# Interleaved pairs of scan tiles, buffers in small pieces, and a table that breaks the planner's ties

## The chip, the cores and the metric

The kernel runs on one NeuronCore of one Trainium2 chip. The metric is the device time of one execution in microseconds (us), the median of several runs. Everything is float32. TensorE (PE in the profile) multiplies matrices into PSUM; VectorE (DVE), ScalarE (ACT) and GpSimd (POOL) work on vectors; SyncE (SP) issues the transfers between the device memory and the on-chip memory SBUF.

## What is computed

Eight images of 384 channels and 1024 positions go through a Mamba-like block and then, the first five of them, through a feed-forward block with binarised weights (the last three have a zero feed-forward output). Cut to what matters:

```
t  = layernorm(x)                               # over the 384 channels, per position
xm, z = split(t @ in_proj_w.T)                  # 768 channels each
xc = silu(causal_conv3(xm))
dt, Bm, Cm = split(xc @ x_proj_w.T, [24, 16, 16])
dt = softplus(dt @ dt_proj_w.T + dt_proj_b)     # 768 channels
h[d,n](l) = exp(dt*A) * h[d,n](l-1) + (dt*xc)[d] * Bm[n](l)   # 768 channels x 16 states
y[d](l)   = sum_n h[d,n](l) * Cm[n](l) + xc*D
x += gelu((y * silu(z)) @ out_proj_w.T @ mlp_w1.T + b1) @ mlp_w2.T + b2
# images 0..4: groupwise sign of the weights, groupwise absmax quantisation
h = quant(layernorm(x) @ sign(W1 - mean) + b1);  x += quant(gelu(h) @ sign(W2 - mean) + b2)
```

## The kernel before

The positions lie along the free dimension of SBUF, channels along the 128 partitions. An image `b` has three stages. `s1` does the norm, the input projections, the convolution and the dt projection, in two halves of 512 positions, and hands `xc`, `z`, `dt`, `dt*xc` (`dtx`) and the rows of B and C to the scan through device memory. `s2` is the scan. `s3` does the output projection and the MLP; `ffn` is the feed-forward block of images 0 to 4, `binarise` its weights.

**The scan.** A tile of 128 partitions holds 32 channels times 4 states (a "quad" `q`, four quads for 16 states). For the six middle images a tile has all 1024 positions; for the first and the last image the halves are done apart, with two groups of channels side by side (`wide` = 2). Two tiles make a unit `m`. In `scan_tile` each tile takes: `exp` on ACT into `da` (PSUM); `u = dtx * B` on POOL (line 886); the scan instruction on DVE (line 890); the product by C, in place on POOL (line 904) or on DVE (line 907), as `on_pool` says; and matmuls with the matrix `fold` (line 842), which sum the states into the PSUM tile `py`. These matmuls are 32 columns wide, and four of them stand side by side in the array. They are issued for two quads at a time, 16 records in the profile (a float32 matmul makes two). `dt_r` and `dtx_r` are loaded with each channel row repeated over four partitions.

**The order.** Nothing is issued by hand. All operations are put into a `Plan` with an engine, a cost, the tiles read and written and a lane; `Plan.run` walks through a model of time, takes for each engine an operation that could start, and emits it. Where several could start, `rank` decides: scan first (lane 0 and the sums in lane -1), then the other stages by lane and image, and within those by the sequence number `op.prio[2]` in which the operations were written down. Each engine then runs its instructions in the order emitted. Where PE would idle for more than 0.7 us in the plan, small matmuls `spare` (line 412) are put in to keep its clock up.

**The buffers.** Each kind of tile has a ring of buffers, and an operation can start only when a buffer is free. The wide ones hold 6 x 512 columns: `front` (2; `xc`, `dt`, `z` of `s1`), `hid` (2; hidden layer of the MLPs), `yg` (1). Silu, softplus and Gelu run over such a tile in one instruction of 3072 columns. `u` has 9 tiles, `dt_r` and `dtx_r` 3 each, `sq` (the square of the norm) 1, `mm` 3 PSUM tiles for all matmul outputs but the scan's. The matmuls of the projections are all emitted by `matmuls` (line 494). `p_dt` (line 722) is the dt projection, 24 real rows padded to 128; `p_bc` (line 703) picks the rows of B and C, in four matmuls of 128 columns, out of `dbc`.

Of the kernel before, what the change touches and what calls it, by code (L numbers as in the profile page):

```python
# [26 lines left out]
F32 = mybir.dt.float32  # L27
# [6 lines left out]
P = 128  # L34
# [8 lines left out]
HK = KH // 2  # L43
T = 512
# [41 lines left out]

def c_act(n):
    return 0.25 + n * 0.00084


def c_dve(n):
    return 0.19 + n * 0.00102


def c_pool(n):
    return 0.18 + n * 0.00214
# [33 lines left out]
class Piece:  # L130
# [8 lines left out]

    def __getitem__(self, part):  # L140
        return self, part

# [20 lines left out]
class Plan:  # L163
# [57 lines left out]
    def run(self):  # L221
# [22 lines left out]
        def choose(e, now, able):  # L244
# [9 lines left out]
            return min(able, key=rank)  # L254

        def rank(op):
# [11 lines left out]
            return (*first, op.prio[2])  # L268
# [83 lines left out]
class Layer:  # L352
    def __init__(self, ctx, tc, a, out):
# [9 lines left out]
        def ring(tag, bufs, where=sbuf):  # L363
# [7 lines left out]
            "front": ring("front", 2), "t_f": ring("t_f", 2), "w_f": ring("w_f", 3),  # L371
            "dbc": ring("dbc", 1), "halo": ring("halo", 2),

            "dt_r": ring("dt_r", 3), "dtx_r": ring("dtx_r", 3), "u": ring("u", 9),
# [4 lines left out]
            "yg": ring("yg", 1), "hid": ring("hid", 2), "t_b": ring("t_b", 1), "w_b": ring("w_b", 3),  # L379
            "w6": ring("w6", 2), "w6_n": ring("w6_n", 2), "res": ring("res", 2),  # L380

            "t_n": ring("t_n", 2), "small": ring("small", 7),
# [9 lines left out]
        for b in range(B):  # L392
            for name in ("dt", "dtx"):
                self.dram[name, b] = handed(f"{name}_d{b}", [DI, L])
# [24 lines left out]

    def constants(self):
# [13 lines left out]
        self.pick = const.tile([P, 2 * NS], F32, name="pick")  # L436
        nc.vector.tensor_add(self.pick, ident[:, DQ : 2 * DQ], ident[:, DP + DQ : DP + 2 * DQ])
        self.edge = const.tile([P, KD, 2], F32, name="edge")
# [50 lines left out]
    def matmuls(self, p, w, t, k0, n, start, stop, r, claim, w0=0):  # L489


        def emit():
            for k in range(n):
                self.nc.tensor.matmul(  # L494
                    p.real, w.real[:, w0 + k, :], t.real[:, k0 + k, :],
# [102 lines left out]
    def s1(self, b):  # L598
# [6 lines left out]
        def by_pair(name, half, t):  # L605
            d = self.dram[name, b]
            self.store(d.real[:, half].rearrange("k p l -> p k l"), t, lambda x: x, [d[half]],
                       4 * P * KD * T)

        def tiled(name, half, t):  # L610
            d = self.dram[name, b]
            to = d.real[:, HALVES[half]].rearrange("(k p) l -> p k l", p=P)
            self.store(to, t, lambda x: x, [d[half]], 4 * P * KD * T)
# [14 lines left out]
        def gate(half, t):  # L628
            z = self.piece(r_z, [P, KD, T], "z")
            for m in range(KD):  # L630
                w = self.weights(r_w, KC, a["in_proj_w"][KD + m])
                pm = self.mm3(w, t, [t[k] for k in range(KC)], [z], "p_z")
                self.affine(
                    lambda m=m, z=z: z.real[:, m, :], lambda pm=pm: pm.real, [pm], [z[m]]
# [637 lines left out]
```

## Time and profile before

| | |
|---|---|
| median of 3 runs | 3261.88 us (3261.76 to 3268.25) |
| profiled execution: time, span | 3262.23 us, 3260.4 us |
| mean granted TensorE clock | 0.984 |
| moved by DMA | 748.73 MB, 230 GB/s |
| first POOL product of the scan starts, last one starts | 105.1 us, 3166.5 us |

The span runs from the first to the last instruction of the program; the time has some 1.8 us more around it. An engine's busy time is the sum of its instructions' durations without overlap. In the rows of the profile, `out<-in` are the program's tile names, `x768` is the count, and behind the bar stand the busy total in us, the mean of one in ns, and the idle time just before with what ended it.

### The profile page before, as it was taken

How to read it: one execution, taken by the hardware profiler on the slowest of the kernel's cores; microseconds unless marked ns; L12 is line 12 of the kernel's file. 1: busy time of each engine (PE TensorE's matmuls, PEld its weight loads, DVE VectorE, ACT ScalarE, POOL GpSimd, SP SyncE). 2: the span in 40 equal slices, each digit the busy share in tenths (PEclk: the TensorE clock that was granted, in tenths of full speed). 3: DMA queues.
4: the chain of work that ended last, by engine and by line, in shares of the span. 5: the costliest groups of instructions: out<-in, count | busy, mean ns of one | idle time of the engine just before them, and what ended most of it. 6: DMA issues, size and time to landing. Idle time of an engine off the chain costs nothing.

```text
span 3260.4 us, 34027 instructions
## 1 busy us (share of the span) xinstructions
PE 3122.5 (96%) x11098; PEld 1317.7 (40%) x11098; DVE 2742.3 (84%) x2127; ACT 2024.3 (62%) x2246; POOL 2848.7 (87%) x1371
## 2 busy tenths in 40 slices
PE   8988999999999999999899999999999999999999
PEld 4333433444433434334334344343443534433334
DVE  4778899799978899888998878999788988789880
ACT  4778787656665576665656566755666565656551
POOL 1688899979999989999989999989999899999970
PEclk9998999999999999999999999999999999999999
DMA  6988778657796568675686667866677656766542
GB/s 218 305 282 276 249 250 294 221 183 234 259 322 197 184 230 291 229 238 197 208 298 211 237 211 246 295 225 226 220 275 250 207 185 205 249 187 207 167 141 76
DMA packets 367345, 748.73 MB, mean 230 GB/s; under 512 B 33856, under 2 KB 111168, under 8 KB 367168
## 3 DMA queue, kind: packets, MB, share of 16 engines
q1 hardware_dynamic: 366736, 746.46, 68.5%
q8 instruction: 89, 1.46, 0.2%
q14 instruction: 88, 0.72, 0.1%
q10 hardware_dynamic: 432, 0.09, 0.0%
HBM read 566.06 MB, written 180.36 MB: 229 GB/s over the span
## 4 chain that ended last, share of the span: by engine, by line
PE 74%; DMA 9%; DVE 6%; ACT 5%; issue 2%; POOL 2%; SPq 1%; ACTq 0%; DVEq 0%; POOLq 0%
PE p_y L494 17%; PE p_o L494 14%; PE p_h L494 13%; PE py L842 9%; PE p_out L494 6%; PE p_z L494 6%; PE p_in L494 5%; DVE da L890 2%; DMA w<-in_out_proj_w 2%; DMA w_f<-in_in_proj_w 2%; DVE u L890 1%; ACT L510 1%; DMA w_b<-in_mlp_w 1%; ACT da L510 1%; PE spare L412 1%
## 5 line engine op out<-in xcount | busy, mean ns | idle before, releaser
L886 POOL TENSOR_TENSOR u<-dtx_r,bc 128x1024 f32<-128x1024 f32 x768 | 1790.4, 2362 | 72.3 <-DMA dtx_r<-dtx_d 46.3
L510 ACT ACTIVATE da<-dt_r,a_neg 128x1024 f32<-128x1024 f32 (+1 forms) x960 | 902.7, 945 | 534.0 <-DVE u L907 331.1
L904 POOL TENSOR_TENSOR u<-u,bc 128x1024 f32<-128x1024 f32 x352 | 828.4, 2364 | 121.5 <-DVE u L890 115.5
L890 DVE TENSOR_TENSOR_SCAN da<-da,u 128x1024 f32<-128x1024 f32 (+1 forms) x416 | 840.5, 2020 | 111.6 <-POOL u L886 62.9
L890 DVE TENSOR_TENSOR_SCAN u<-da,u 128x1024 f32<-128x1024 f32 (+1 forms) x352 | 699.5, 2010 | 90.3 <-ACT da L510 63.0
L494 PE MATMUL p_h<-t,w_b 128*128 128x512 f32 x1152 | 513.6, 600 | 10.9 <-DMA w_b<-in_mlp_w 9.9
L907 DVE TENSOR_TENSOR u<-da,bc 128x1024 f32<-128x1024 f32 x416 | 507.9, 1221 | 10.5 <-ACT state L901 0.3
L494 PE MATMUL p_o<-g,w 128*128 128x512 f32 x1152 | 506.7, 595 | 5.4 <-ACT g L510 2.9
L842 PE MATMUL py<-u,fold 128*32 128x512 f32 x3072 | 376.6, 605 | 4.5 <-DVE u L907 4.5
L494 PEld LDWEIGHTS p_h<-t,w_b 128*128 128x128 f32 x1152 | 214.7, 190 | 298.1 <-issue 256.4
L494 PEld LDWEIGHTS p_o<-g,w 128*128 128x128 f32 x1152 | 215.9, 190 | 292.0 <-issue 277.3
L494 PE MATMUL p_y<-tn,w_b 128*128 128x512 f32 x720 | 324.9, 598 | 4.0 <-DVE tn L592 3.3
L494 PE MATMUL p_y<-gf,w_n 128*128 128x512 f32 x720 | 319.0, 599 | 6.7 <-DMA w_n<-bin_w 4.0
L510 ACT ACT_TABLE_LOAD x222 | 284.8, 1283 | 11.7 <-DVE xc L661 7.3
L494 PE MATMUL p_out<-yg,w 128*128 128x512 f32 x552 | 249.2, 604 | 8.9 <-DMA w<-in_out_proj_w 4.3
L494 PE MATMUL p_z<-t,w_f 128*128 128x512 f32 x504 | 232.5, 611 | 8.2 <-DMA w_f<-in_in_proj_w 6.2
L494 PE MATMUL p_in<-t,w_f 128*128 128x512 f32 x504 | 228.3, 602 | 10.8 <-DMA w_f<-in_in_proj_w 8.6
L494 PEld LDWEIGHTS p_y<-gf,w_n 128*128 128x128 f32 x720 | 135.1, 191 | 187.6 <-issue 172.4
L494 PEld LDWEIGHTS p_y<-tn,w_b 128*128 128x128 f32 x720 | 133.9, 190 | 183.9 <-issue 155.4
L842 PEld LDWEIGHTS py<-u,fold 128*32 128x32 f32 x3072 | 81.5, 110 | 261.1 <-issue 203.2
L525 ACT ACTIVATE g<-p_h,v_vecs 128x512 f32<-128x512 f32 x157 | 106.3, 681 | 120.9 <-PE p_h L494 120.7
L525 ACT ACTIVATE y<-p_y,v_vecs 128x512 f32<-128x512 f32 x138 | 94.1, 683 | 130.0 <-PE p_y L494 100.3
(112 smaller groups left out, 2700.3 us busy)
## 6 DMA issues: line engine op xcount, KB each, us to landing
dtx_r<-dtx_d SPq DMA_DIRECT2D x144, 512.0 KB, 5.8
dt_r<-dt_d SPq DMA_DIRECT2D x144, 512.0 KB, 6.0
w_b<-in_mlp_w SPq DMA_DIRECT2D x192, 192.0 KB, 2.9
w<-in_mlp_w SPq DMA_DIRECT2D x96, 384.0 KB, 3.6
w_f<-in_in_proj_w SPq DMA_DIRECT2D x168, 192.0 KB, 4.2
y_d<-y SPq DMA_DIRECT2D x120, 256.0 KB, 3.4
gf<-y_d SPq DMA_DIRECT2D x20, 1536.0 KB, 9.5
xc_d<-xc SPq DMA_DIRECT2D x16, 1536.0 KB, 7.3
```

The lines of the kernel that those rows point to most:

```text
L412: self.plan.fill = lambda: self.nc.tensor.matmul(self.plan.spare.real[:, : 2 * P], self.ones, self.one.to_broadcast([P, 2 * P]), start=Tru ...
L494: self.nc.tensor.matmul(p.real, w.real[:, w0 + k, :], t.real[:, k0 + k, :], start=start and k == 0, stop=stop and k == n - 1,)
L510: lambda: self.nc.scalar.activation(out(), in_(), func, **{k: v() if callable(v) else v for k, v in kw.items()}),
L525: nc.scalar.activation(out(), in_(), AF.Identity, bias=bias, scale=scale)
L842: nc.tensor.matmul(py.real[p0 : p0 + DQ, :], self.fold, hc, start=False, stop=(q == NQUAD - 1), skip_group_check=True,)
L886: add("POOL", 2.36, lambda: nc.gpsimd.tensor_mul(u.real, dtx_r.real, spread(bq)), r=[dtx_r, bq], w=[u])
L890: add("DVE", (0.2 if half else 0.15) + n * 0.00209, lambda k=k, col=col: nc.vector.tensor_tensor_scan(to.real[:, k, :], da.real[:, k, :], ...
L904: add("POOL", 2.36, lambda: nc.gpsimd.tensor_mul(u.real, u.real, spread(cq)), r=[cq], w=[u])
L907: add("DVE", 1.21, lambda: nc.vector.tensor_mul(u.real, da.real, spread(cq)), r=[da, cq], w=[u])
```

## The change

- **Interleaved pairs.** A unit's two tiles become one pair. `u` and `dtx_r` hold `[128, n, 2]`, the two tiles' values alternating; `s1` writes `dtx` to device memory in this form. One POOL instruction multiplies the pair by the row of B, repeated for both (step 0 in the innermost dimension), one more by the row of C. DVE's scan reads `u` with a step of two elements, and writes it so where C is multiplied on POOL; where C is multiplied on DVE, that product is written with a step of two. The `fold` matmuls read `u` with a step of two. For the last quad the product is written over `dtx_r` itself. Channels are grouped so that a pair's two tiles are in the same partitions of neighbouring 128-row blocks (the weights are laid out on the host to suit). `on_pool` changes which quads have C multiplied on POOL.
- **Small pieces.** `front`, `hid` and `yg` become rings of pieces of 2 x 512 columns (`Split`): 7, 6 and 3 of them. Silu, softplus, Gelu, clip, stores and loads go piece by piece. `res` goes from 2 to 4, `u` from 9 tiles to 3 pairs, `dtx_r` from 3 tiles to 2 pairs, `small` from 7 to 5.
- **Projections.** `p_bc` is replaced by one matmul with the matrix `join`, which gives the dt rows twice, at partitions 0 and 32, and the rows of B and C in one block that one DMA stores. The dt projection then uses 32 rows of the array per matmul, two at a time. `binarise` sums the weights in four column strips and reduces by group on DVE.
- **Ties.** `rank` adds to the sequence number a number between -16 and 16, made from it and from an entry of `TURNS`, one per 100 us of planned time; where the entry is 0, nothing is added.

```diff
+STRETCH, REACH = 100, 16
+TURNS = (
+    0, 0, 0, 7221, 34335, 0, 0, 0, 0, 0, 13486, 57910,
+    29230, 27985, 0, 0, 0, 0, 13021, 0, 59942, 28281, 23998, 0,
+    35936, 26840, 53796, 0, 0, 45431, 13885,
+)
+def turned(n, by):
+    x = ((n + 1) * 2654435761 + by * 40503 * 65537) & 0xFFFFFFFF
+    x = ((x ^ x >> 15) * 2246822519) & 0xFFFFFFFF
+    return (x ^ x >> 13) % (2 * REACH + 1) - REACH
...
+def c_pair(n):
+    return 0.19 + n * 0.00188
...
+class Split:
+    def __init__(self, make, n, per):
+        self.pieces, self.per = [make() for _ in range(n // per)], per
+    def at(self, k):
+        return self.pieces[k // self.per].real[:, k % self.per, :]
+    def __getitem__(self, k):
+        return self.pieces[k // self.per][k % self.per]
...
-            return min(able, key=rank)
-
-        def rank(op):
+            at = int(now / STRETCH)
+            turn = TURNS[at] if at < len(TURNS) else 0
+            return min(able, key=lambda op: rank(op, turn))
+        def rank(op, turn):
...
-            return (*first, op.prio[2])
+            return (*first, op.prio[2] + (turned(op.prio[2], turn) if turn else 0))
...
-            "front": ring("front", 2), "t_f": ring("t_f", 2), "w_f": ring("w_f", 3),
+            "front": ring("front", 7), "t_f": ring("t_f", 2), "w_f": ring("w_f", 3),
...
-            "dt_r": ring("dt_r", 3), "dtx_r": ring("dtx_r", 3), "u": ring("u", 9),
+            "dt_r": ring("dt_r", 3), "dtx_r": ring("dtx_r", 2), "u": ring("u", 3),
...
-            "yg": ring("yg", 1), "hid": ring("hid", 2), "t_b": ring("t_b", 1), "w_b": ring("w_b", 3),
-            "w6": ring("w6", 2), "w6_n": ring("w6_n", 2), "res": ring("res", 2),
-
-            "t_n": ring("t_n", 2), "small": ring("small", 7),
+            "yg": ring("yg", 3), "hid": ring("hid", 6), "t_b": ring("t_b", 1), "w_b": ring("w_b", 3),
+            "w6": ring("w6", 2), "w6_n": ring("w6_n", 2), "res": ring("res", 4),
+            "t_n": ring("t_n", 2), "small": ring("small", 5),
...
+        def in_place(t, func, table):
+            parts = [t[k] for k in range(KD)]
+            for p, piece in enumerate(t.pieces):
+                mine = parts[p * PER : (p + 1) * PER]
+                self.act(lambda piece=piece: piece.real, lambda piece=piece: piece.real, func,
+                         c_act(PER * T), r=parts if p == 0 else mine, w=mine, table=table)
...
+            p_all = self.piece("mm", [P, T], "p_all")
+            n_all = DP + 2 * NS
+            add("PE", MM, lambda dbc=dbc, p_all=p_all: nc.tensor.matmul(
+                p_all.real[:n_all, :], self.join, dbc.real, start=True, stop=True
+            ), r=[dbc], w=[p_all])
             self.affine(
-                lambda rows=rows: rows.real, lambda p_bc=p_bc: p_bc.real, [p_bc], [rows], n=TG
+                lambda dbc=dbc: dbc.real[:n_all, :], lambda p_all=p_all: p_all.real[:n_all, :],
+                [p_all], [dbc],
             )
             d = self.dram["rows", b]
-            for g in range(G):
-                at = slice(cols.start + g * TG, cols.start + (g + 1) * TG)
-                self.store(d.real[:, at], rows, lambda x, g=g: x[g * DQ : (g + 1) * DQ, :],
-                           [d[half, g]], 4 * DQ * TG)
-            dt = self.piece(r_x, [P, KD, T], "dt")
-            for k in range(KD):
-                if k % KC == 0:
+            self.store(d.real[:, cols], dbc, lambda x: x[DP:n_all, :], [d[half]], 4 * 2 * NS * T)
...
+                def two(k=k, pds=pds, dbc=dbc, ws=ws):
+                    for i in range(2):
+                        rows = slice(i * DQ, (i + 1) * DQ)
+                        nc.tensor.matmul(
+                            pds[i].real, ws[i].real[rows, (k + i) % KC, :], dbc.real[rows, :],
+                            start=True, stop=True,
+                        )
+                add("PE", MM + 0.2, two, r=[dbc, *dict.fromkeys(ws)], w=pds, claim=[dt.pieces[k // PER]])
...
+            d = self.dram["dtx", b]
+            for p in range(KC):
+                dtx = self.piece("sq", [P, T, 2], "dtx")
+                add("POOL", 2.35, lambda p=p, dtx=dtx, xc=xc, dt=dt: nc.gpsimd.tensor_mul(
+                    dtx.real.rearrange("p n i -> p i n"), xc.pieces[p].real, dt.pieces[p].real
+                ), r=[xc[2 * p], xc[2 * p + 1], dt[2 * p], dt[2 * p + 1]], w=[dtx])
+                self.store(d.real[p, :, half * L : (half + 1) * L], dtx,
+                           lambda x: x.rearrange("p n i -> p (n i)"), [d[p, half]], 4 * P * L)
...
+            dtxs = self.piece("dtx_r", [P, wide, n, 2], "dtx_r")
+            d = self.dram["dtx", b]
+            at = 2 * cols.start
+            for x in range(wide):
+                src = d.real[p, r0 + x :: G, at : at + 2 * n].unsqueeze(1)
+                load(dtxs[x], lambda x=x, t=dtxs: t.real[:, x].rearrange("p n i -> p (n i)"),
+                     src.to_broadcast([DQ, SQ, 2 * n]), [d[p, h] for h in halves], 8 * P * n)
...
+                u = dtxs if q == NQUAD - 1 else self.piece("u", [P, wide, n, 2], "u")
...
+                        parts = [u.real[:, 0, h, i] for i in both for h in HALVES] if (
+                            half is None) else [u.real[:, x, :, i] for i in both for x in both]
+                        for g, hc in enumerate(parts):
                             nc.tensor.matmul(
-                                py.real[p0 : p0 + DQ, :], self.fold, hc,
+                                py.real[g * DQ : (g + 1) * DQ, :], self.fold, hc,
                                 start=False, stop=(q == NQUAD - 1), skip_group_check=True,
...
-    def on_pool(self, i, q, m):
-
-        return q == 0 or (q == 2 and (i == 0 or m % 3))
...
+    def on_pool(self, q, m):
+        return q % 2 == 0 or (q == 1 and m % 4 == 0)
...
+        def product(t, x, row):
+            nc.gpsimd.tensor_mul(
+                u.real[:, x], t.real[:, x], row.real.unsqueeze(2).to_broadcast([P, n, 2])
             )
-        add("POOL", 2.36, lambda: nc.gpsimd.tensor_mul(u.real, dtx_r.real, spread(bq)),
-            r=[dtx_r, bq], w=[u])
-        to = u if on_pool else da
-        for k, col in enumerate(cols):
-            add("DVE", (0.2 if half else 0.15) + n * 0.00209, lambda k=k, col=col: nc.vector.tensor_tensor_scan(
-                to.real[:, k, :], da.real[:, k, :], u.real[:, k, :],
-                state.real[:, col : col + 1] if half else 0.0, ALU.mult, ALU.add,
-            ), r=[da, u] + ([state[cols[0]]] if half else []), w=[to])
-        if half == 0:
-            c0, step = cols[0], cols[1] - cols[0]
-            kept, last = lambda: state.real[:, c0 : c0 + step + 1 : step], n - 1
-            if on_pool:
-                add("POOL", 0.2, lambda: nc.gpsimd.tensor_copy(kept(), to.real[:, :, last]),
-                    r=[to], w=[state[c0]])
-            else:
-                add("ACT", 0.16, lambda: nc.scalar.copy(kept(), to.real[:, :, last]),
-                    r=[to], w=[state[c0]])
+        for x in range(wide):
+            add("POOL", c_pair(2 * n), lambda x=x: product(dtxs, x, bq), r=[dtxs[x], bq],
+                w=parts[x])
...
+            to = (lambda i: in_u(i)) if on_pool else (
+                lambda i, da=da: da.real[:, i, :])
+            for i, col in enumerate(mine):
+                add("DVE", (0.2 if half else 0.15) + n * 0.00209, lambda i=i, col=col, to=to,
+                    da=da, in_u=in_u: nc.vector.tensor_tensor_scan(
+                        to(i), da.real[:, i, :], in_u(i),
+                        state.real[:, col : col + 1] if half else 0.0, ALU.mult, ALU.add,
+                    ), r=[da, u[t]] + ([state[col]] if half else []),
+                    w=[u[t] if on_pool else da])
...
+                def by_dve(t=t, da=da):
+                    row = cq.real.unsqueeze(1)
+                    if wide == 1:
+                        nc.vector.tensor_mul(u.real[:, 0, :, t], da.real[:, 0, :], cq.real)
+                    else:
+                        nc.vector.tensor_mul(
+                            u.real[:, t].rearrange("p n i -> p i n"), da.real,
+                            row.to_broadcast([P, wide, n]),
+                        )
+                add("DVE", 1.21, by_dve, r=[da, cq], w=[u[t]])
         if on_pool:
-            add("POOL", 2.36, lambda: nc.gpsimd.tensor_mul(u.real, u.real, spread(cq)),
-                r=[cq], w=[u])
-        else:
-            add("DVE", 1.21, lambda: nc.vector.tensor_mul(u.real, da.real, spread(cq)),
-                r=[da, cq], w=[u])
+            for x in range(wide):
+                add("POOL", c_pair(2 * n), lambda x=x: product(u, x, cq), r=[cq], w=parts[x])
...
+    def gelu(self, g, k0, r=(), **kw):
+        parts = [g[k] for k in range(k0, k0 + HK)]
+        for i in range(0, HK, PER):
+            piece = g.pieces[(k0 + i) // PER]
+            mine = parts[i : i + PER]
+            self.act(lambda piece=piece: piece.real, lambda piece=piece: piece.real, AF.Gelu,
+                     c_act(PER * T), r=[*r, *(parts if i == 0 else mine)], w=mine, table="gelu", **kw)
...
+            for k in range(0, HK, PER):
+                need = [g[i * HK + k + j] for j in range(PER)]
+                self.matmuls(po, w, g, i * HK + k, PER, i + k == 0, i * HK + k + PER == KH, need,
+                             claim, k)
...
-                        pm.real, self.ones, w.real[:, k - ks.start, :],
-                        start=(k == 0), stop=(k == kt - 1),
+                        pm.real[g * DQ : (g + 1) * DQ, :], self.ones[:, :DQ],
+                        w.real[:, k - ks.start, :], start=(k < lanes), stop=(k >= kt - lanes),
                     )
-            add("PE", (ks.stop - ks.start) * MM, total, r=[w], w=[pm])
+            add("PE", 0.25 + MM, total, r=[w], w=[pm])
```

## The prediction

> **What bounds the kernel now.** I read the busy totals first, then the busy times between the first and the last product of the scan, then the chain of waits, then the rows of the scan by shape.
>
> ```profile
> PE 3122.5 (96%) x11098; PEld 1317.7 (40%) x11098; DVE 2742.3 (84%) x2127; ACT 2024.3 (62%) x2246; POOL 2848.7 (87%) x1371
> ```
>
> Four engines are nearly full at once, so the ends of the run have to be cut off before a bound can be named. By the tile `u`, the first POOL product of the scan starts at 105.1 us and the last one ends at 3168.9 us. Before that the scan has no input; after it TensorE alone works off the last half. The middle is 3064 us. The first line below is all work in it (span, then PE, PEld, DVE, ACT, POOL), the second only PE's fillers `spare`, which the planner puts where PE would idle:
>
> ```profile
> 105.00:3169.00 3064.00, 2944.28 (x10441) 1233.20 (x10440) 2689.96 (x2058) 1956.25 (x2166) 2836.08 (x1353) 0.98 0.70 234
> ```
> ```profile
> 105.00:3169.00 3064.00, 71.20 (x286) 53.20 (x286) 0.98 0.70 234
> ```
>
> POOL fills 2836/3064 = 92.6% of the middle and DVE 87.8%. PE's busy time less the fillers is 2873 us (93.8%), too much, since the ends of matmuls are modelled. The end of the chain gives PE's real rate:
>
> ```profile
> 3194.70 30.90 PE p_h L494 x72
> 3225.60 30.91 PE p_o L494 x72
> ```
> ```profile
> 2773.19 1.85 PE py L842 x16
> 2775.05 8.03 PE spare L412 x36
> ...
> 2784.93 2.37 PE spare L412 x10
> ```
>
> A record of 512 full-width columns takes 30.90/72 = 0.429 us, a group of 16 `py` records 1.85. The program has 5664 full records (p_h, p_o 1152 each, p_y 1440, p_in, p_z, p_out 576 each, p_dt 192): 2431 us; 192 `py` groups: 355; x_proj 44; the small ones about 90. That is 2920, of which some 72 lie in the head and 78 in the tail, so 2770 in the middle, 90.4%. **PE and POOL bound the middle together**: neither is idle for long, and each waits for the other in turn. The fillers at 2775 show it: no matmul was ready while the scan was behind. The waits of POOL show the coupling from its side (us in total, times, longest):
>
> ```profile
> POOL u L904 <- DVE u L890: 115.5, 70, 10.6
> ...
> POOL u L886 <- DMA dtx_r<-dtx_d: 46.3, 14, 17.8
> ...
> POOL u L886 <- PE py L842: 21.6, 11, 5.3
> ```
>
> The prices of the scan and of the two matmul stages that change (busy, mean ns):
>
> ```profile
> L886 POOL TENSOR_TENSOR u<-dtx_r,bc 128x1024 f32<-128x1024 f32 x768 | 1790.4, 2362 | 72.3 <-DMA dtx_r<-dtx_d 46.3 <-PE py L842 21.6 <-issue 2.4
> L904 POOL TENSOR_TENSOR u<-u,bc 128x1024 f32<-128x1024 f32 x352 | 828.4, 2364 | 121.5 <-DVE u L890 115.5 <-PE p_in L494 1.0 <-POOL u L886 0.6
> ...
> L907 DVE TENSOR_TENSOR u<-da,bc 128x1024 f32<-128x1024 f32 x416 | 507.9, 1221 | 10.5 <-ACT state L901 0.3
> ...
> L732 POOL TENSOR_TENSOR xc<-xc,dt 128x512 f32<-128x512 f32 x96 | 118.6, 1275 | 18.1 <-ACT dt L510 15.6 <-ACT state L901 2.5
> ...
> L722 PE MATMUL p_dt<-dbc,w_f 128*128 128x512 f32 x168 | 81.9, 620 | 9.5 <-ACT dt L525 6.0 <-ACT rows L523 3.4
> ```
>
> **What the Trainium skill says.** "GPSIMD Engine Reference", section 3.1, puts a two-input elementwise product at about 2.6 cycles an element because both operands share one read port; the trace's 2.362 us for 1024 agrees in kind. Its section 7 lets reads slow down by half only where the step exceeds 8 bytes; the pairs step by exactly 8. No run yet shows it. "SBUF — State Buffer", section "Door 1: The DMA port swizzle", says that two hits in a 16-byte line keep full speed, so a float32 step of two is free for DVE and PE reads; the trace has no such operand. "TensorEngine Tiling (Array Packing)", section "Key Properties", says that tiles run independently and that a change of mode drains: 16 `py` records in 1.85 us instead of 16 x 0.429 = 6.9 agree with the first half.
>
> **POOL.** One product now covers two tiles, interleaved element by element, with the row of B or C repeated for both. Counted in pairs there are 384 first products. Second products on POOL go from 352 tiles to 218 pairs (q = 0 and 2 always, q = 1 for every fourth m: 27 a batch for six batches, 14 a half for the four halves). So 602 pairs replace 1120 tiles = 2619 us. A pair's price is in no row. Upper bound: two old ones, 4.72. Lower bound, an estimate: reads fall from two to one and a half per element if the repeated value is fetched once, 0.75 x 4.72 = 3.54. I take the middle, 4.13; the constant in the diff (0.19 + 0.00188 x 2048 = 4.04) lies by it, and the old POOL constants (2.36, and 1.276 for 512 elements) match their rows. 602 x 4.13 = 2486: **133 us less**. Break-even is 2619/602 = 4.35. The dt-by-x products go from 96 x 1.275 to 48 x about 2.36 (-9); splitting the clips adds some 2, the edge about 2. POOL's middle: about 2698.
>
> **DVE.** Products by C fall from 416 tiles to 2 x 166 = 332: 84 x 1.221 = **-103 us**. Scans keep number and size; their strided operand I cost at nothing by the page above (bounds: -0, +10% of the 2090 us of scans = +209). Middle: about 2587.
>
> **PE.** dt projections: 96 matmuls of two records become 48 pairs on two row strips. Side by side they save 48 x 2 x 0.429 = 41; a drain of some 0.2 a pair takes back 10; net -31 (bounds -41 and, if not side by side, +10). `p_bc` gives way to one 512-column matmul: 16 x 0.858 - about 7 = +7. The weight sums of binarise on four column strips: 42 records, 18 us busy, to about 9. **PE: -33**, so 2737 in the middle.
>
> **ACT, DMA, buffers.** Silu, softplus and Gelu in pieces of 1024: 96 + 64 + 40 = 200 more instructions. From 2.765 us for 3072 and 1.476 for 1536, an instruction's fixed part is 0.19: +37 us on an engine 62% busy. In exchange the first matmul of p_o or p_y2 needs one piece and not six. DMAs per half of s1: four stores become twelve, four row stores one, one dt weight more; with yg, gf and half as many dtx loads, SP issues 96 + 28 + 40 - 120 = +44 on some 1900, and at 0.60 us each, as the head's chain shows, that is 26 us spread over SP's 3260; bytes hardly change. SP's in-order queue passes loads between finer stores, so no load waits behind 1.5 MB for its data. New waits: `u` has three pairs where it had nine tiles, with `dtx_r` itself as the fourth, held until PE's sums; behind a late sum stands POOL's next product, and behind that both scans. Also dtx goes through the single `sq` buffer, so the norm's square queues behind three stores. POOL's gap to PE (3064 - 2698 = 366 us) covers these at first; with that cover gone they cost what the 21.6 us row costs now, a few times over.
>
> **The sum.** The fullest engine now fills 92.6% of the middle. With POOL (-5%) and DVE (-4%) relieved, PE is the fullest alone. At 92.6% its 2737 us need 2956; had I taken the busy count, 2873 - 33 = 2840 at 95% needs 2989. I take 2970, 94 less than now: 33 of work, 61 of waits, less than the 71 of fillers. The head may lose 5, as the first dtx load needs one 512 KB piece; the tail of 91 stays: 100 + 2970 + 91 = 3161. The profiled execution had a span of 3260.4 and a time of 3262.23; that 1.8 gives **3163 us** against the median of 3261.88. The table of ties only permutes neighbours (sequence number ± 16 inside one stage and batch); I cost it at nothing, -20 to +20.
>
> **The rivals.**
> 1. *PE alone, no wait comes back.* The waits are PE's own latencies, short and everywhere, not POOL's lateness. For it: most idle of PE's weight loads is "issue". Then 3262 - 33 = 3229.
> 2. *The pair is no cheaper (slower).* POOL reads twice what the estimate says. At 4.72 POOL's middle is 2836 + 222 = 3058, because 84 tiles more were moved to it; at 97% filled 3153, so 3350, at today's 92.6% 3500. It decides from about 4.4 us a pair. Against it: the shared read port, and constants that match.
> 3. *The 8-byte step costs PE or DVE (slower).* If `py` ran at half rate, 192 x 1.85 = +355 on PE; scans by a tenth, +209 on DVE. 3350 and more. Against it: the page on SBUF.
> 4. *It doesn't do what it says.* Shallower `u` and the shared `sq` put POOL into waits that eat the 94 us: about 3262.
>
> **How the numbers follow.** A measurement of this kernel can tell about 0.2% (6.5 us) from no change. Forecast 66% (own range 3105 to 3215), rival 1 14%, rival 2 10%, rival 3 6%, rival 4 4%. Faster 0.80, same 0.04, slower 0.16. The range goes from 3095, where PE is 95% full and the table helps, to 3262, which takes in rival 1 and most of 4 and leaves out rivals 2 and 3.
>
> **What would show it.** Right: POOL products of 128x2048 near 4.1 us; POOL's busy total near 2710 and DVE's near 2640; `py` groups still 1.85 us and scans still 2.28; p_dt pairs starting together; fillers well under 80 us; PE's share of the chain above 74%. Wrong: a pair above 4.35 us, POOL waiting for `py` by over 60 us, or fillers unchanged with PE's work down by 33.

## The result and the profile after

The changed kernel takes **3276.87 us** (median of 18 runs, 3262.95 to 3284.95) against 3266.61 for the kernel before on the same chip (18 runs): ratio 1.0028, interval 1.0016 to 1.0040. It is slower by 0.3%, where the prediction said 3163. The profiled execution took 3273.15 us with a span of 3271.4, 11.0 us longer than before.

The busy totals of the changed kernel, from its page:

```profile
PE 3101.8 (95%) x10900; PEld 1274.5 (39%) x10900; DVE 2669.0 (82%) x2092; ACT 2013.2 (62%) x2389; POOL 2724.9 (83%) x1025
```

POOL lost 124 us and DVE 73, nearly as forecast, and PE 21. The span did not follow. The middle (first to last product of the scan) now runs from 96 to 3194, cut in the same way as before: all work, then the fillers alone.

```profile
96.00:3194.00 3098.00, 2946.43 (x10320) 1201.62 (x10321) 2623.53 (x2017) 1953.00 (x2311) 2713.92 (x1007) 0.98 0.70 233
```
```profile
96.00:3194.00 3098.00, 48.40 (x180) 33.43 (x180) 0.98 0.70 233
```

The middle is 34 us longer, at 3098, although POOL fills only 87.6% of it (2713.92/3098), where it filled 92.6%. Fillers fell from 71 to 48 us. The head is 9 us shorter and the tail 14 shorter. The rows of the scan by shape (busy, mean ns):

```profile
L931 POOL TENSOR_TENSOR u<-dtx_r,bc 128x2048 f32<-128x2048 f32 x216 | 881.3, 4091 | 163.1 <-PE py L896 90.8 <-issue 61.0 <-DMA bc<-rows_d 5.2
L956 DVE TENSOR_TENSOR_SCAN u<-da,u 128x1024 f32<-128x1024 f32 x324 | 738.7, 2283 | 118.7 <-POOL u L931 55.5 <-ACT da L555 53.9 <-DVE u L956 0.9
...
L931 POOL TENSOR_TENSOR u<-u,bc 128x2048 f32<-128x2048 f32 x162 | 661.6, 4088 | 58.1 <-DVE u L956 56.8 <-PE py L896 1.1
...
L787 POOL TENSOR_TENSOR dtx<-xc,dt 128x1024 f32<-128x1024 f32 x48 | 113.9, 2374 | 69.7 <-DMA dtx_d<-dtx 39.6 <-ACT dt L555 24.4 <-ACT z L555 2.7
```

A pair costs 4.09 us (4.13 was taken; 4.27 as two products of 1024 in the first and the last image), and a scan with its step of two still 2.28. Now the chain that ended last, in order of time (start, us, what), in the stretch the prediction showed:

```profile
2745.53 1.94 PE py L896 x16
2747.47 4.55 PE spare L450 x20
...
2762.32 1.94 PE py L896 x16
```

A `py` group takes 1.94 us, where it took 1.85. The chain's shares by engine, before and then after:

```profile
PE 74%; DMA 9%; DVE 6%; ACT 5%; issue 2%; POOL 2%; SPq 1%; ACTq 0%; DVEq 0%; POOLq 0%
```
```profile
PE 74%; DMA 15%; DVE 4%; ACT 3%; POOL 2%; issue 2%; SPq 1%; ACTq 0%; DVEq 0%; POOLq 0%
```

PE keeps its 74%; DMA goes from 9 to 15%. The waits of PE say which transfers (us in total, times, longest), before and after:

```profile
PE p_h L494 <- DMA w_b<-in_mlp_w: 9.9, 6, 2.8
PE p_in L494 <- DMA w_f<-in_in_proj_w: 8.6, 6, 6.4
PE p_in L494 <- DMA w_b<-in_in_proj_w: 6.3, 1, 6.3
...
PE p_z L494 <- DMA w_f<-in_in_proj_w: 6.2, 4, 2.7
```
```profile
PE p_z L539 <- DMA w_f<-in_in_proj_w: 38.1, 17, 6.6
PE p_h L539 <- DMA w_b<-in_mlp_w: 18.1, 9, 4.5
PE p_in L539 <- DMA w_f<-in_in_proj_w: 14.3, 8, 3.7
PE p_o L539 <- DMA w<-in_mlp_w: 10.4, 8, 2.5
```

Waits for `w_f` and `w_b` in these rows went from 31.0 us in 17 waits to 70.5 in 34. Such a wait costs more than its length. The timeline of PE around one of them (start, us, and in brackets the idle time before):

```profile
68.28 1.25 PE L772 MATMUL p_dt<-dbc,w_f 32*128 32x512 f32 x4
73.37 8.17 PE L539 MATMUL p_z<-t,w_f 128*128 128x512 f32 x12 [3.85 <-DMA w_f<-in_in_proj_w]
```

Twelve records take 12 x 0.429 = 5.1 us at PE's rate; after 3.85 us of waiting they took 8.2, since the first six started 0.85 us apart. The granted TensorE clock goes with this: in the views of two stretches below (start and end, length, busy time of each engine) it is the third number from the end, 0.50 in the first and 1.00 in the second.

```profile
73.40:77.50 4.10, 4.10 (x5) 1.79 (x6) 0.00 (x0) 1.57 (x2) 2.12 (x1) 0.50 0.79 254
...
79.00:81.60 2.60, 2.60 (x7) 1.14 (x6) 0.56 (x1) 0.02 (x1) 0.10 (x1) 1.00 1.03 366
```

In the trace before, the clock stood at 0.50 for 107 us of the span, in the trace after for 138; apart from the very end, every such stretch lies beside a wait of PE. The number of full-width records that followed one another in them 0.853 us apart, without a wait, rose from 41 to 65.

**Where the 11 us come from.** I add, over all records of PE, the time from one start to the next, and split off what exceeds the record's own rate by over 0.4 us as a wait (us; with the lines drawn a little otherwise the differences shift by up to 5):

| | before | after | |
|---|---|---|---|
| waits for w_f, w_b | 33.5 | 77.6 | +44 |
| waits for other transfers | 27.7 | 43.2 | +16 |
| waits for engines | 84.4 | 61.2 | -23 |
| p_dt | 88.5 | 55.9 | -33 |
| p_sums; p_all less p_bc | 17.8; 5.3 | 5.6; 14.6 | -3 |
| py | 356.1 | 370.9 | +15 |
| p_z, p_h, p_o (15 of the 18 at a clock of 0.50) | 1266.2 | 1284.0 | +18 |
| fillers `spare` | 75.0 | 51.8 | -23 |

The rest is within 3 us in any row, `p_in`, `p_out` and `p_y` included; all rows together make the 11.

### The profile page after: what moved, and what is told of

Same layout as the page of the kernel before. It is cut to its first block, busy times and chain, and to the rows that moved or that the text cites. A ratio compares the mean times of both kernels' runs of the same rounds, so it can differ in the third digit from the quotient of the medians.

```text
span 3271.4 us, 33608 instructions
## 1 busy us (share of the span) xinstructions
PE 3101.8 (95%) x10900; PEld 1274.5 (39%) x10900; DVE 2669.0 (82%) x2092; ACT 2013.2 (62%) x2389; POOL 2724.9 (83%) x1025
## 4 chain that ended last, share of the span: by engine, by line
PE 74%; DMA 15%; DVE 4%; ACT 3%; POOL 2%; issue 2%; SPq 1%; ACTq 0%; DVEq 0%; POOLq 0%
PE p_y L539 17%; PE p_o L539 13%; PE p_h L539 13%; PE py L896 10%; PE p_out L539 7%; PE p_z L539 6%; PE p_in L539 5%; DMA w_f<-in_in_proj_w 4%; DMA dtx_r<-dtx_d 2%; DMA w_b<-in_mlp_w 1%; DMA w<-in_mlp_w 1%; POOL u L931 1%; DVE u L956 1%; PE p_dbc L741 1%; DMA w_n<-bin_w 1%
## 5 line engine op out<-in xcount | busy, mean ns | idle before, releaser
L931 POOL TENSOR_TENSOR u<-dtx_r,bc 128x2048 f32<-128x2048 f32 (+1 forms) x360 | 1185.9, 3310 | 194.8 <-PE py L896 107.2
L931 POOL TENSOR_TENSOR u<-u,bc 128x2048 f32<-128x2048 f32 (+1 forms) x274 | 900.5, 3291 | 110.6 <-DVE u L956 105.2
L956 DVE TENSOR_TENSOR_SCAN u<-da,u 128x1024 f32<-128x1024 f32 (+1 forms) x436 | 867.9, 2006 | 138.6 <-POOL u L931 68.3
L539 PE MATMUL p_o<-g,w 128*128 128x512 f32 x1152 | 514.0, 598 | 10.4 <-DMA w<-in_mlp_w 10.4
L956 DVE TENSOR_TENSOR_SCAN da<-da,dtx_r 128x1024 f32<-128x1024 f32 (+1 forms) x192 | 386.9, 2019 | 45.0 <-POOL dtx_r L931 28.7
L931 POOL TENSOR_TENSOR dtx_r<-dtx_r,bc 128x2048 f32<-128x2048 f32 (+1 forms) x120 | 396.8, 3311 | 2.6
L896 PE MATMUL py<-u,fold 128*32 128x512 f32 x2304 | 299.7, 621 | 0.0
L956 DVE TENSOR_TENSOR_SCAN da<-da,u 128x1024 f32<-128x1024 f32 (+1 forms) x140 | 285.1, 2043 | 10.4 <-ACT da L555 5.7
L539 PE MATMUL p_z<-t,w_f 128*128 128x512 f32 x504 | 246.4, 639 | 38.1 <-DMA w_f<-in_in_proj_w 38.1
L976 DVE TENSOR_TENSOR dtx_r<-da,bc 128x1024 f32<-128x1024 f32 x144 | 175.1, 1223 | 3.2
```

Of the source, the lines that this page charges most:

```text
L539: self.nc.tensor.matmul(p.real, w.real[:, w0 + k, :], t.at(k0 + k), start=start and k == 0, stop=stop and k == n - 1,)
L896: nc.tensor.matmul(py.real[g * DQ : (g + 1) * DQ, :], self.fold, hc, start=False, stop=(q == NQUAD - 1), skip_group_check=True,)
L931: nc.gpsimd.tensor_mul(u.real[:, x], t.real[:, x], row.real.unsqueeze(2).to_broadcast([P, n, 2]))
L956: da=da, in_u=in_u: nc.vector.tensor_tensor_scan(to(i), da.real[:, i, :], in_u(i), state.real[:, col : col + 1] if half else 0.0, ALU.mult ...
L976: nc.vector.tensor_mul(u.real[:, 0, :, t], da.real[:, 0, :], cq.real)
```

## The experiments

Times are medians; each ratio is to the kernel before on the same chip, and the changed kernel's own is 1.0028. One per cent is 33 us. Several kernels multiply stale weights or sum without C, as their expectations say.

| run | us | ratio, interval |
|---|---|---|
| e1_swap | 3300.17 | 1.0112, 1.0095 to 1.0128 |
| e2_no_table | 3281.35 | 1.0055, 1.0038 to 1.0072 |
| e3_no_weight_loads | 3163.83 | 0.9700, 0.9685 to 0.9714 |
| e4_no_pool_c | 3268.76 | 1.0018, 1.0007 to 1.0029 |
| e5_before_no_weight_loads | 3215.93 | 0.9851, 0.9827 to 0.9875 |
| e6_before_no_pool_c | 3250.60 | 0.9957, 0.9939 to 0.9975 |
| e7_py_contiguous | 3268.77 | 1.0016, 1.0004 to 1.0028 |
| e8_weights_on_act_queue | 3264.65 | 1.0006, 0.9992 to 1.0021 |
| e9_weights_ring_five | 3308.92 | 1.0127, 1.0104 to 1.0150 |
| e10_pieces_undone | 3352.89 | 1.0248, 1.0215 to 1.0282 |
| e11_before_weights_on_act_queue | 3298.19 | 1.0087, 1.0059 to 1.0115 |
| e12_ring_five_act_queue | 3345.64 | 1.0245, 1.0214 to 1.0275 |
| e13_weights_unwaited | 3308.06 | 1.0151, 1.0132 to 1.0171 |
| e14_before_weights_unwaited | 3288.03 | 1.0088, 1.0073 to 1.0103 |
| e15_w_f_on_act_queue | 3268.96 | 1.0032, 1.0015 to 1.0050 |
| e16_dt_one_strip | 3296.00 | 1.0098, 1.0076 to 1.0120 |
| e17_weights_aside | 3202.09 | 0.9817, 0.9796 to 0.9837 |
| e18_weights_tiny | 3184.92 | 0.9756, 0.9735 to 0.9778 |

### Is POOL a bound? (e4, e6)

```diff
-  add("POOL", c_pair(2 * n), lambda x=x: product(u, x, cq), r=[cq], w=parts[x])
+  add("POOL", c_pair(2 * n), lambda: None, r=[cq], w=parts[x])
```

> The changed kernel in the same order, but the products by C that GpSimd does are left out (218 pairs, some 890 us of GpSimd), so the results differ. The prediction's own reasoning (GpSimd relieved, TensorE finds work ready): GpSimd's busy total falls to about 1830 us and the time by 40 to 80 us. Theory D: under 25 us, since the weights come no sooner. Theory P: under 10 us.

> The kernel before, order unchanged, with the 352 products by C on GpSimd left out (y is summed without C there). GpSimd loses 828 us of work. If GpSimd and TensorE bound the middle together, as the prediction said, the middle becomes TensorE's alone: 3130 to 3200. If TensorE with its transfers is the bound before too (as the run of the changed kernel without these products suggests, 8 us), 3245 to 3262.

The changed kernel with 888 us of POOL's work taken out is 3 us quicker (0.1%; the intervals overlap), the kernel before with 815 us taken out 14 us. The freed POOL mostly waits for the sums, first in e4, then in e6:

```profile
POOL u L931 <- PE py L896: 797.9, 135, 14.9
```
```profile
POOL u L886 <- PE py L842: 498.2, 95, 13.3
```

In these orders POOL does not bound either kernel together with PE; most of what it gains it spends waiting for PE. Both runs keep the order that was planned with POOL's full cost; what a new order would make of a freer POOL was not run. This is the step on which the forecast rested.

### What the weight loads cost (e3, e5, e17, e18, e13, e14)

e3 and e5 leave out the loads of the weight rings after the first of each buffer. The edit is in the function that loads all four rings, so it takes in the 384 KB loads of `w6` and `w6_n` besides those of `w_f` and `w_b` (192 KB), which most of the expectations name. The same holds for the other runs of this part and for e8, e11 and e12.

```diff
-  self.load(w, lambda t: t, src, r=r, size=4 * P * k * P, cost=0.34)
+  def emit():
+      if len(kept) < w.ring.bufs:
+          kept.append(w.real); self.nc.sync.dma_start(w.real, src)
+  self.plan.add("SP", 0.34, emit, r=r, w=[w], size=4 * P * k * P)
```

> The changed kernel in the same order, but each weight ring of the matmuls is loaded only until its buffers are full once; later matmuls use the weights that are there, so the results differ and some 170 of 750 MB are not moved. This takes away every wait of TensorE for a weight load. Theory D: the time falls by 60 to 110 us, to 3165 to 3215, near what the sum of the prediction gave. Theory P: by under 30 us, to 3245 or more; the waits move to the scan.

> The kernel before, order unchanged, with every 192 KB load into w_f and w_b after the first three of each ring left out (stale weights are multiplied). The changed kernel lost 113 us to 3164 by the same edit. Theory W (the changed kernel's saved work went into waits for weights): the kernel before waited 33 us for them by the waits of PE and not 88, so it gains only 50 to 80, to 3185 to 3215, and without weight loads the changed kernel is ahead by 20 to 50. Rival N (weights cost both kernels alike): 113 less, 3150, and the changed kernel is no better without them either.

The changed kernel gains 3.3% (107 us), the one before 1.5% (49 us): without weight loads the changed kernel is 52 us ahead. So the change does have a gain, and the weight loads take it, and 10 us more. In e3, PE's waits fall by 88 us in the split of the table, and its other time by some 25, most of it `p_z`. That e3 lands on 3163.83, the number of the forecast, is chance: the forecast kept the loads.

Do the loads cost by their bytes or by being waited for? e13 and e14 sent all later loads into one buffer that no matmul reads.

> The changed kernel, order unchanged, with all its weight loads issued, but after the first of each ring into one buffer that no matmul reads (the matmuls use the first, stale weights). Traffic is whole, waiting gone. Theory W (it is TensorE's waiting): near the run without the loads, 3160 to 3190. Rival T (it is the traffic, which delays the loads of dtx, dt and the stores): 3230 to 3270. Between the two, both share it.

> The same edit in the kernel before. Theory W: near its run without the loads, 3210 to 3235, so 40 to 60 behind the changed kernel with the same edit. Rival T: 3245 to 3262, and no more than 20 from the changed kernel's.

Both became slower, because SyncE then had to finish each load before it could issue the next. Its waits in e13:

```profile
SPq L544 <- DMA w_f<-in_in_proj_w: 336.4, 120, 8.0
SPq L544 <- DMA w_b<-in_mlp_w: 336.3, 140, 8.3
```

They decide nothing on the question, and show that a queue held up this way costs 29 to 40 us by itself. e17 and e18 ask it again, each with another branch in `emit`:

```diff
+      else:  # e17: 16 areas in device memory in turn
+          self.nc.sync.dma_start(to[:, : k * P], src.rearrange("p k o -> p (k o)"))
```
```diff
+      else:  # e18: one partition's row
+          self.nc.sync.dma_start(w.real[0:1], src[0:1])
```

> The changed kernel, order unchanged, whose weight loads after the first of each ring go from device memory to 16 areas set aside in device memory, which nobody reads (the matmuls use the first, stale weights). The bytes are still moved, but neither TensorE nor SyncE waits for anything in them. Theory W (waiting, TensorE's for the loads and SyncE's for free buffers): near the run without the loads, 3160 to 3190. Rival T (the traffic delays the other transfers): 3225 to 3270.

> The changed kernel, order unchanged, whose weight loads after the first of each ring move one partition's row (1.5 or 3 KB) and not all 128 (stale weights are multiplied). SyncE still waits for the buffer and TensorE for the load, but the bytes are gone. If SyncE's order and its standing behind TensorE's buffers cost the time: 3240 to 3275, hardly better than the changed kernel. If what costs is that a load of 192 KB lands 4 to 6 us after its issue: the loads land in about 2 us, TensorE's waits for w_f and w_b fall from 75 us to under 20, and the time to 3165 to 3200.

With the bytes and no wait, the time falls by 2.1% (69 us); with the waits and no bytes, by 2.7% (89 us). Of the 107 us that the loads cost, 69 go when nothing waits for them. The other 38 or so point to the traffic's effect on other transfers, as far as e17 can tell, whose bytes end in device memory and not in SBUF: PE waits 96 us for engines, 67 in e3, and ACT and POOL wait 60 and 81 us for transfers, 20 and 30 in e3. The two edits overlap, so their gains do not add. e18, in which SyncE still stands behind TensorE's buffers, is 18 us above e3, so this standing costs little by itself. PE's waits in e18 for the tiny loads:

```profile
PE p_z L554 <- DMA w_f<-in_in_proj_w: 9.6, 4, 6.0
...
PE p_h L554 <- DMA w_b<-in_mlp_w: 6.6, 5, 2.0
...
PE p_in L554 <- DMA w_f<-in_in_proj_w: 5.3, 4, 3.1
```

That is 21.5 us against 70.5. So most of the cost is that the bytes arrive several us after their issue: those of `in_proj` into `w_f` 4.7 us in the median (4.2 before), those of `w_f` and `w_b` that TensorE waited for 6.0.

### Can the loads be made earlier? (e1, e8, e15, e11, e9, e12)

e1 held each 1 MB load of `dtx_r` back until the next store of `yg` was issued.

```diff
+  if late is not None:
+      self.held.append((late, lambda: nc.sync.dma_start(view(), src)))
...
-  self.rows_moved(zr, rows_of(d), lambda at, mem: nc.sync.dma_start(mem, at),
+  self.rows_moved(zr, rows_of(d), lambda at, mem: (nc.sync.dma_start(mem, at), self.release()),
```

> The changed kernel with one thing moved: the 1 MB load of dtx_r is issued just behind the next store of yg and not just ahead of it; plan, order of all other instructions and all work are the same. Theory D (late weights: the 1 MB load stands ahead of the yg store, the next zr load has to wait for that store to land, and the weight loads queue behind it in SP's order): the yg store lands in about 3 us and not 6, SP's wait on it falls from 140 to about 45 us, TensorE's idle time before weight loads from some 100 to some 60 us, and the time falls by 30 to 60 us, to about 3215 to 3245. Theory P (TensorE's own work and short waits set the time): within 8 us of the changed kernel. Theory T (the table fitted the plan to a model of transfers that is too fast): within 15 us, since the plan is the same.

SyncE's wait behind the `yg` store fell from 140.2 us to this:

```profile
SPq L864 <- DMA yg_d<-zr: 35.5, 24, 6.2
```

TensorE's waits for weights stayed (32.8, 21.4 and 15.5 us for p_z, p_h and p_in), and the kernel lost 27 us. The order of the store and the large load is not the cause of these waits; why the kernel lost 27 us was not traced.

e8 and e11 issue the loads of all weight rings from ScalarE (712 in e8, 508 of them of `w_f` and `w_b`), e15 those of `w_f` alone.

```diff
-  self.load(w, lambda t: t, src, r=r, size=4 * P * k * P, cost=0.34)
+  self.plan.add("SP", 0.34, lambda: self.nc.scalar.dma_start(w.real, src), r=r, w=[w], size=4 * P * k * P)
```

> The changed kernel, order unchanged, whose weight loads into w_f and w_b are issued by ScalarE and not by SyncE. Theory Q (weights come late because SyncE issues in order and stands 140 us behind the y*z products before a store): the waits of TensorE for w_f and w_b fall from 88 to under 40 us and the time to 3225 to 3255. Rival L (the transfers themselves take 4.7 us and ring depth of three is too short): waits stay at 70 to 100 and the time within 10 of 3277, or above it, since ScalarE now stands behind buffers to be freed.

> The changed kernel, order unchanged, with only the 224 loads of w_f issued by ScalarE. All 508 on ScalarE took 12 us off and left new waits of TensorE for ScalarE (dbc, z, mean; some 20 us more). If half of the loads bring most of the relief (waits for w_f 57 us to under 15) and half of the new waits, 3250 to 3262, better than both kernels; if the relief is only exchanged for waits, 3265 to 3277.

> The kernel before, order unchanged, with its w_f and w_b loads issued by ScalarE. In the changed kernel this edit took 12 us. Theory W (late weights are special to the changed kernel, 75 us of TensorE's idle against 32): here it brings 0 to 6, 3257 to 3264. Rival N (any order gains by it alike): 12 less, near 3250.

PE's waits in e8:

```profile
PE p_h L540 <- DMA w_b<-in_mlp_w: 12.2, 11, 2.5
...
PE p_z L540 <- DMA w_f<-in_in_proj_w: 6.2, 5, 1.7
PE p_in L540 <- DMA w_f<-in_in_proj_w: 5.5, 4, 2.3
```

By the split of PE's records, waits for weights fell from 77.6 to 28.8 us, and waits for engines rose from 61.2 to 100.5: ScalarE itself now stands behind buffers. The net is 7 us (the intervals overlap), a tie with the kernel before. e15 brings nothing measurable. The same edit costs the kernel before 28 us, where neither theory allowed a loss. So issue by SyncE does make loads late in the changed kernel (by its order, or by the queue shared with the other transfers: the edit changes both), but moving them exchanges one wait for another.

e9 has five buffers in `w_f` and `w_b`, and a new order; e12 adds ScalarE's issue.

```diff
-  "front": ring("front", 7), "t_f": ring("t_f", 2), "w_f": ring("w_f", 3),
+  "front": ring("front", 6), "t_f": ring("t_f", 2), "w_f": ring("w_f", 5),
```

> The changed kernel with five buffers in each of w_f and w_b in place of three, paid for with one piece of front (7 to 6) and one res (4 to 3); the planner makes a new order. Its groups of six matmuls take 2.57 us, so three buffers give a transfer some 5.1 us from the freeing of a buffer to its use, and the transfers that TensorE waited for took 6.0 us (median). Theory D (the ring is too shallow for these transfers): five buffers give 10 us, the waits of TensorE for w_f and w_b fall from 75 to under 25, and the time to 3200 to 3245, although the planner's own end is 73 us later (3209 for 3137). Rival Q (SyncE's order makes them late): the waits stay above 50 and the time at 3265 to 3330.

> The kernel with five buffers for w_f and w_b and, besides, the weight loads issued by ScalarE. Under theory D nothing is left to gain by the other queue: within 8 of the run with five buffers alone. Under rival Q it is 10 to 30 below that run. If both add up it is the fastest version, at 3190 to 3230.

The waits went as theory D said, to 9.1 us. The time did not: 3309, because waits for engines (115 us), for other transfers (67) and fillers (80) took their place. The planner's order is looser with one piece of `front` less; the run can't say how much of the loss is that. e12 is worse than e9. Neither theory's time was right.

### The parts of the change (e2, e10, e7, e16)

```diff
-TURNS = (0, 0, 0, 7221, 34335, ...)
+TURNS = ()
```

> The changed kernel with an empty table of ties; everything else is the same, the planner orders anew. In the planner's own model the table is worth 37 us (PE's last operation ends at 3137 with it, at 3174 without). Theory T: the gain exists only in the model, so the time is within 12 us of the changed kernel or below it. Theories D and P: the table is worth what the model says, the time rises by 25 to 40 us to about 3300 to 3315.

The table is worth 0.27%, 9 us, with intervals that overlap a little, so hardly clear of noise; theory T was right. The planner's own model gives it 37 (its plan ends at 3137 with it, at 3174 without).

e10 makes `PER` 6, `front` and `hid` two tiles, `yg` one:

```diff
-PER = 2
+PER = 6
```

> The changed kernel with the small pieces undone (front, hid and yg again in tiles of 6 x 512 columns, 2, 2 and 1 of them) and without the table; the interleaved pairs and the new projections stay. It stands against the run without the table, 3281. If the finer pieces bring the waits for weights (more transfers in SyncE's order, 2253 for 2089), the waits of TensorE for w_f and w_b fall from some 75 us to 35 and the time to 3225 to 3265. If the pieces are a gain that the weights hide, the time rises to 3300 to 3350, as the planner's own end does (3241 for 3174). If neither, 3270 to 3295.

Against e2 it loses 63 us. The small pieces are a gain; the pairs and projections without them are slower than the kernel before. The fillers alone, in e10's middle:

```profile
96.00:3270.00 3174.00, 148.63 (x628) 116.59 (x628) 0.98 0.68 227
```

149 us of fillers for 48 mean that in this order PE often has no matmul ready. Waits for weights are lower, at 49 us; that they grow where PE's other gaps are closed is a reading of this, not shown by itself.

e7 lets the sums read runs of neighbouring elements:

```diff
-  parts = [u.real[:, 0, h, i] for i in both for h in HALVES] if ( ...
+  flat = u.real.rearrange("p x n i -> p (x n i)")
+  parts = [flat[:, k * T : (k + 1) * T] for k in range(4)]
```

> The changed kernel, order unchanged, whose sums read u in runs of 512 neighbouring elements and not with a step of two (they sum the wrong elements). If the step costs the 82 ns by which a group of 16 py records grew, the group falls from 1.94 to 1.85 us, 192 groups give 16 us, and the time falls by 10 to 20 to about 3260, since TensorE is the bound. If the growth has another cause (the DVE and GpSimd accesses beside it), the groups stay at 1.94 and the time at 3277.

A group on the chain of e7:

```profile
2700.97 1.85 PE py L896 x16
```

The step of two is the cause of the 82 ns. All `py` records fall from 370.9 to 357.4 us. The time falls by some 4 (1.0028 to 1.0016, overlapping). Between the two traces the span falls by 0.8 only, and the 13.5 us did not come back as waits: PE sat idle for 165 us in the changed kernel and for 168 in e7. The granted clock stood at 0.50 for 164 us in e7 and for 138 in the changed kernel (means 0.975 and 0.979), and `p_in` alone took 9 us more. Why it did so is open.

e16 puts both matmuls of a dt pair in one strip:

```diff
-  rows = slice(i * DQ, (i + 1) * DQ)
+  rows = slice(0, DQ)
```

> The changed kernel, order unchanged, whose two matmuls of a dt projection pair use the same 32 rows of the array and not two strips. If the strips run side by side (a pair 1.06 us when nothing is waited for, 1.33 in the median), the pair rises to 1.72 or more, 48 pairs x 0.4 to 0.65 = 20 to 30 us, and the time to 3285 to 3305. If the pair is bound by its wait for two of the three PSUM tiles `mm`, as the rest of the expected gain suggests, the pairs' sum of 93 us rises by under 15 and the time stays within 8 of 3277.

Without their waits the pairs take 95.3 us for 55.9, and the time rises by 23, as expected. The strips do run side by side, and of 39 us of work added to PE 23 show in the time.

## Why the prediction was wrong, point by point

- **POOL's work: right.** 4.09 us a pair, busy total 2725 (2710 forecast); rival 2 is out. The Trainium skill's page "GPSIMD Engine Reference", section 7, lets reads slow down only beyond a step of 8 bytes. I took the pairs for such a step, but their products on POOL read `u` and `dtx_r` in order, so no run here tests it.
- **DVE: right.** The products by C fell by 104 us (103 forecast) and the scans cost nothing more; the total fell by only 73, as DVE got more of the copies out of PSUM (`z`, `xc`, `dt` and `g`, +22). The Trainium skill's page "SBUF — State Buffer", "Door 1: The DMA port swizzle", gives full speed to two hits in a 16-byte line, and a DVE scan with a step of two agrees (2.28 us).
- **PE, the three terms named: right.** p_dt -33 (-31 forecast; two strips took 1.06 us, the 0.86 plus 0.2 of the sum), p_sums -12 (-9), p_all +9 (+7).
- **PE, the step of two at nothing: wrong in size.** I carried the same section over to PE's reads, and there the trace does not agree: +15 us, of which e7 takes 13.5 back. Rival 3 named the place, at 24 times the price.
- **PE, the clock after waits: missing.** +18 us on `p_z`, `p_h` and `p_o`, 15 of them in records that started at half rate at a granted clock of 0.50. With these two terms PE's work without waits and fillers falls by some 3 us, not 33.
- **"PE and POOL bound the middle together", 61 us of waits given back: this step failed.** POOL's 92.6% was taken for a bound. e6 takes out over six times as much as the change does and gains 14 us. The waits of PE that engines release fell by 23 us; I gave back 61 without asking which of PE's waits a freer POOL could end. Rival 1 had this half right (the waits were not POOL's lateness), but it kept the 33 us of work.
- **"No load waits behind 1.5 MB": wrong side of the ledger.** I counted SyncE's issues (26 us, spread) and not when a weight load would be needed. PE's waits for transfers rose by 60 us, and this ate the rest of the gain. The kernel before already showed 31 us of waits for `w_f` and `w_b`; they should have been a rival.
- **What the fillers said.** They fell as forecast, from 71 to 48 us, but were replaced by waits for transfers. "Fillers well under 80" proved nothing.
- **Rival 4** (buffers eat the gain, 3262) was the nearest in time. POOL did wait 108 us for `py`, 22 before, the sign named as wrong; but e4 shows that these waits cost next to nothing.

Still open: why more loads come late. I match each `w_f` load with the last reader of its buffer, by order. The late ones (25, 10 before) were issued some 2.3 us after their buffer came free (0.4 before) and landed 6.6 us later (5.8 before), medians. While the late loads of `w_f` and `w_b` were under way, the 16 DMA engines were 92% busy (97% before); for the other loads of these rings it was 73% (72%), and they landed in 3.5 us (3.4). So the late ones met bursts of other transfers. Over the whole span the share hardly changed, 70% for 69%, and why twice as many loads met a burst just when PE needed them is not shown. No run separated a denser order of PE's groups from SyncE's order without bringing other waits. No kernel that keeps the whole computation beat the kernel before; e8 ties with it.

## What to carry to other kernels

An engine that is 93% busy is a bound only if taking its work away moves the end: leave its instructions out once, in the same order, before you design around it. When the true bound is one engine, look in its own waits for what ends last; here more of them ended with transfers that landed some 6 us after their issue. Look at the granted clock beside each wait too: a wait may cost more than its length. A cheaper instruction elsewhere may be paid for by the bound engine, here by a strided read.

## What the runs showed of the hardware

- `py` matmuls (four 32-column strips, float32) that read their moving operand with a step of two elements start 4% further apart: a group of 16 records takes 1.936 us for 1.854. DVE scans with that step do not change (2.28 us).
- A GpSimd product of 2048 elements with a row repeated in the innermost step takes 4.09 us, two of 1024 without it 4.72.
- Two float32 matmuls of 512 columns take 1.06 us together on two strips of 32 rows, 1.91 in one strip, and 1.82 as two full-width matmuls (medians where nothing was waited for). The strips paid only side by side.
- Beside waits of PE, the granted TensorE clock stood at 0.50 for stretches of 3.41 us or a multiple of it (6.83, 10.24, 17.07). Full records started 0.853 us apart in them and 0.429 elsewhere.
